# State-space layers: two more states weighed on TensorE and ScalarE, a block's first statistics on GpSimd, and the next decay first in each slot

## The chip, the cores and the metric

The kernel runs on one core of a Trainium2 chip, as one launch. The core has five engines that work beside each other, each through its own queue in order: TensorE (PE in the profile: matrix products and transposes, into PSUM), VectorE (DVE), ScalarE (ACT), GpSimd (POOL), and the sync engine (SP), which here only issues DMAs. The metric is the device time of the launch in microseconds (us), lower is better. The kernel before took 2108.87 us (median of three runs, 2108.46 to 2109.21).

## The reference, cut to what matters

The network has four layers of two halves each. The change is in one half only, the first half of layer 1 (names in l1a): four state-space layers one after another, on 4 sequences of 256 tokens (1024 columns after the batch is regrouped), with 256 inner channels and 16 states. In each of them:

```
xz = layer_norm(x) @ Wi.T;  xs, z = split(xz)
u  = silu(conv4(xs) + cb)
dt, Bc, Cc = split(u @ Wx.T);  dt = softplus(dt @ Wdt.T + bdt)
step t:  h = exp(dt[t]*A) * h + dt[t]*B[t]*u[t]      # 256 channels x 16 states
         y[t] = sum over states of h * C[t]
y = (y + u*Dp) * silu(z);  x = x + y @ Wo.T
```

All is float32. The 16 states of a channel are independent until the sum over states that gives y.

## The kernel before, in words

The tokens are worked on in four blocks of 512, and the four layers give 16 **blocks** in all (class Job, `jobs`; 128 channels lie on the partitions, two halves c of the channels, 512 tokens in the free dimension). A block has 16 **slots**, one for each state s. The loop over `slots` (L1077) writes the order of PE, DVE, ACT and POOL out by hand (`manual_schedule`); what stands before the loop is ordered by the scheduler. In slot s of a block:

- `decay` (L972, ACT, two instructions of 128x510) writes the decays of the *next* state into one of two PSUM buffers `das`; it waits until the scan two before has read that buffer.
- `inflow` (L966, POOL, 128x1024) makes the scan's input three slots ahead, in a buffer of the tag st; `weigh` (L999, POOL, the same size) multiplies a scanned state by its row of C.
- `scan` (L977, DVE) is the recurrence of the state, 128x1024, in place.
- The sum over states has two ways. An odd state is *turned* (`turn`, L986 to L993): half of its columns is transposed by four PE instructions into the single PSUM bank "acc", and two DVE instructions of 128x256 multiply by C, which is then a value per partition, and add into `yt`. One half is done one slot after the scan and one half two slots after, so that each slot has one set of four transposes and one pair of DVE instructions; for s = 1 ACT does them (L991). An even state is weighed by POOL and added on PE into the PSUM tile `yacc` (`add_up`, L1008, two matmuls of 128x512 with the identity); ADD gives the slot of that. State 8 is turned too, by EXTRA, through the bank "mm", in slot 10 and slot 0 of the next block. So nine states are turned and seven weighed. `tail` (L1010) adds `yt` into `yacc` by PE, multiplies by the gate and projects.
- `front` (L831) is the next but one block's preparation, a generator of some 40 steps. Two are taken per slot, from slot 6 of one block to slot 9 of the next: one at the head of the slot (before decay), one near its end. Its PE work stands in the second of a slot's steps, and ACT reads the result in the first step of the following slot. All go through one PSUM bank, "mm". By slot: statistics of the layer norm (DVE, slot 6) with two small VectorE instructions L849 and L850, then the reciprocal root on POOL (L854 to L859, slot 9), normalization (ACT L864, slot 10), transposes (PE L869, slot 11), the convolution as matmuls with shifted inputs (L880, in slots 12 and 13 for half the channels and 14 and 15 for the others), read by ACT (L885) in slots 14 and 0, Silu of u and of the gate with their table loads (L888, L949, slot 0), B, C and dt (L895 to L913, slots 1 to 4), z (L929, slots 5 and 6), and the softplus and dt*u (L936 to L943, slots 7 to 9).

Before the loop, block 0's front is run whole, the other blocks' outer layer norms are done, and at the loop's first pass block 1's front is started with 20 steps at once (L1081 to L1084).

PSUM has eight banks: one "mm", one "acc", two buffers of decays of two banks each, and `yacc` of two.

Of the kernel before, what the change touches and what calls it, by code (L numbers as in the profile page):

```python
# [9 lines left out]
F32 = mybir.dt.float32  # L10
BF16 = mybir.dt.bfloat16
U32 = mybir.dt.uint32
AF = mybir.ActivationFunctionType
ALU = mybir.AluOpType
AX = mybir.AxisListType

P = 128
B, S, D = 8, 256, 128
NTB = 4
TB = 512  # L20
# [4 lines left out]
NL, DI, DS, DR = 4, 256, 16, 8  # L25
# [5 lines left out]
EPS = 1e-5  # L31
# [143 lines left out]
def network_kernel(ctx: ExitStack, tc: tile.TileContext, x_in, packs, places, conv_w, out, stages=STAGES):  # L175
    nc = tc.nc
    V, A, G, T = nc.vector, nc.scalar, nc.gpsimd, nc.tensor
# [25 lines left out]
    xs = []  # L203
# [9 lines left out]
    for tb in range(1, NTB):  # L213
        load_x(tb)
    ident, ones, part, headmask, tri, run, iota, first = (
        K(n) for n in ("ident", "ones", "part", "headmask", "tri", "run", "iota", "first"))
# [7 lines left out]
    def layer_norm(src, name, dst=None):  # L224

        gen = norm(src, name, dst)
        while True:
            try:
                next(gen)
            except StopIteration as end:  # L230
                return end.value
# [52 lines left out]
    def ts(i, n=P):  # L284
        return slice(i * n, (i + 1) * n)
# [488 lines left out]
    def l1a(w0):  # L774
# [7 lines left out]
        LEAD = 26  # L782
        AHEAD = 3
        Q = 2
        with ExitStack() as es:
# [3 lines left out]
            pool = es.enter_context(tc.tile_pool(name="l1a", bufs=2))  # L789
            tmp = es.enter_context(tc.tile_pool(name="l1a_t", bufs=1))  # L790
            big = es.enter_context(tc.tile_pool(name="l1a_b", bufs=5))
# [39 lines left out]
            def front(job):  # L831
# [14 lines left out]

                rt = sm.tile([P, 4, NT], F32, tag="rt", name=f"rt_{n}")
                r0, v, t, nm = (rt[:, j] for j in range(4))
                V.tensor_scalar(v, mv[:, :, 1], EPS, None, ALU.add)  # L849
                V.tensor_scalar(nm, mv[:, :, 0], -1.0, None, ALU.mult)  # L850

                for _ in range(6):
                    yield
                G.tensor_tensor(r0, v, mhalf, ALU.pow)  # L854
                G.tensor_tensor(t, v, r0, ALU.mult)
                G.tensor_tensor(t, t, r0, ALU.mult)
                G.tensor_scalar(t, t, -0.5, 1.5, ALU.mult, ALU.add)
                G.tensor_tensor(r0, r0, t, ALU.mult)
                G.tensor_tensor(nm, nm, r0, ALU.mult)  # L859
                yield  # L860
                yield
                xn = tk.tile([P, NT, D], F32, tag="xn", name=f"xn_{n}")
# [98 lines left out]

            def inflow(job, s):

                job.st[s] = t = big.tile([P, 2, TB], F32, tag="st", name=f"st_{job.n}_{s}", bufs=14)
                row = job.rows_b[s // Q][:, s % Q, :]
                G.tensor_tensor(t, job.du, row.unsqueeze(1).to_broadcast([P, 2, TB]), ALU.mult)  # L966

            def decay(job, s):
                da = das[s % 2]
                for c in range(2):  # L970
                    k = c * DS + s
                    A.activation(seq(da[:, c, :])[:, :, 1:], seq(job.dt[:, c, :])[:, :, 1:], AF.Exp,  # L972
                                 scale=rates[job.l][:, k : k + 1])
# [2 lines left out]
                st = flat(job.st[s])  # L976
                V.tensor_tensor_scan(st, flat(das[s % 2]), st, 0.0, ALU.mult, ALU.add)  # L977

            def turn(job, s, half, kind="acc"):

                st = job.st[s]
                ps = mm_tile(f"tr_{job.n}_{s}_{half}", kind)
                for j in range(2):
                    i = 2 * half + j
                    for c in range(2):
                        T.transpose(ps[:, j * DI + c * P : j * DI + (c + 1) * P], st[:, c, ts(i)], ident)  # L986
                for j in range(2):
                    i = 2 * half + j
                    src, dst, cs = ps[:, ts(j, DI)], job.yt[:, i, :], job.ct[:, i, s : s + 1]
                    if s == 1:  # L990
                        A.activation(dst, src, AF.Copy, scale=cs)  # L991
                    else:
                        V.scalar_tensor_tensor(dst, src, cs, dst, ALU.mult, ALU.add)  # L993
# [34 lines left out]
            jobs = []  # L1028
# [8 lines left out]
            def slot(g):  # L1037
                return slots[g] if 0 <= g < len(slots) else (None, 0)

            layer_norm(xs[0], "l1a0", ys[0])  # L1040
            for _ in front(jobs[0]):
                pass
            for tb in range(1, NTB):
                layer_norm(xs[tb], f"l1a{tb}", ys[tb])

            def rows_of(g):

# [15 lines left out]

            EXTRA = {10: (0, 8, 0), 0: (1, 8, 1)}
            ADD = {0: 9, 2: 10, 4: 11, 6: 12, 10: 14, 12: 16, 14: 18}
            adds = {}
            for g, (job, s) in enumerate(slots):
                if s in ADD:  # L1070
                    adds[g - s + ADD[s]] = job, s
            gens, fronts = {}, []
            step = lambda what: next(gens.get(what, iter(())), None)

            kinds = mybir.EngineType
            with tc.manual_schedule(engines={kinds.PE, kinds.DVE, kinds.Activation, kinds.Pool}):
                for g in range(len(slots) + 10):  # L1077
                    job, s = slot(g)

                    nxt = slot(g + LEAD)  # L1080
                    if nxt[0] and (g == 0 or nxt[1] == 0):  # L1081
                        fronts.append(front(nxt[0]))
                        for _ in range(2 * nxt[1]):
                            next(fronts[-1])  # L1084
                    for gen in fronts:
                        next(gen, None)
                    if job:
# [4 lines left out]

                        rows_of(g + 3 * Q)
                        rows_from(g + 2 * Q)
                    nxt = slot(g + 1)
                    if nxt[0]:
                        decay(*nxt)
                    if slot(g + AHEAD)[0]:
                        inflow(*slot(g + AHEAD))
                    if job:  # L1100
# [6 lines left out]
                    if j2 and s2 in ADD:  # L1107
                        weigh(j2, s2)
                    at = g % DS
                    if at in EXTRA:  # L1110
                        j2 = slot(g - DS * EXTRA[at][0])[0]
                        if j2:
                            turn(j2, *EXTRA[at][1:], "mm")
                    if at == 7:
                        step("tail")
                    if job and s == 8:
# [446 lines left out]
```

## Time and profile before

| what | value |
|---|---|
| median of three runs | 2108.87 us |
| the profiled execution: its time, its span | 2106.59 us, 2104.8 us |
| busy share of the span: PE, DVE, ACT, POOL | 75%, 80%, 51%, 60% |
| first scan starts, last scan ends | 376.9 us, 1394.3 us |
| a block in the middle (705.4 to 769.0) | 63.6 us: DVE 60.2 busy, POOL 54.4, PE 46.3, ACT 41.7 |
| scans L977 | 256 of 2280 ns |
| turns' DVE instructions L993 | 512 of 469 ns |
| inflow L966, weighing L999 (POOL) | 256 of 2356 ns, 112 of 2355 ns |

The profile has one line for a group of instructions (source line, engine, operation, output and inputs by name, shapes, count, busy us and mean ns, idle time before them and what ended it). A timeline has one line for a run of like instructions: start, duration, engine, line, operation, tiles, count, and in brackets the idle time of that engine before it with what released it. A matmul in float32 that is no transpose is issued twice, so that a product of 128x512 has two rows. PE's busy time is modelled at the ends; the distance between starts says more. The time stands 1.8 us above the span in the profiled execution, and the median of the runs 2.3 us above that time.

### The profile page before, as it was taken

To read this page: it belongs to the slowest core of one execution; us is meant where nothing else is said; L and a number is where in the kernel's file an instruction comes from. 1 tells how busy PE (TensorE), PEld (TensorE's weight loads), DVE (VectorE), ACT (ScalarE), POOL (GpSimd) and SP (SyncE) were. 2 spreads that over 40 slices of the span, in tenths; PEclk is the share of its full clock that TensorE was granted. 3 is DMA by queue.
4 is the path that set the end of the run, shared out by engine and by line. 5 is a ranking of instruction groups with operands and counts; after the bars stand their busy time and mean duration, and the time that the engine had idled before them with its cause. 6 is when DMAs were issued, how large, how long until landed. Compare 5 with 4: busy or idle time off the path is not lost. (4 is left out here: it accounts for less than half of the span.)

```text
span 2104.8 us, 21141 instructions
## 1 busy us (share of the span) xinstructions
PE 1585.9 (75%) x6829; PEld 946.2 (45%) x6829; DVE 1674.1 (80%) x3020; ACT 1077.4 (51%) x1759; POOL 1257.9 (60%) x887
## 2 busy tenths in 40 slices
PE   4989875587767787777776668679999867694775
PEld 1434332243433443433443334444455667583665
DVE  6776446699999999999999999973555558799996
ACT  2655333675566765666755667433221335353442
POOL 1000002898889988889888899941242544837356
PEclk8999997688889888789888889799999989786887
DMA  4000002233223332233223333300020524320000
GB/s 127 1 1 1 0 29 91 90 102 113 99 92 123 102 107 95 92 113 112 102 98 95 105 103 104 108 0 0 0 72 13 185 92 158 91 73 9 6 6 5
DMA packets 67693, 153.27 MB, mean 73 GB/s; under 512 B 5248, under 2 KB 26368, under 8 KB 67328
## 3 DMA queue, kind: packets, MB, share of 16 engines
q1 hardware_dynamic: 60224, 123.79, 17.6%
q0 software_dynamic: 7360, 28.14, 4.2%
q8 instruction: 54, 0.88, 0.2%
q14 instruction: 55, 0.45, 0.1%
HBM read 142.74 MB, written 9.18 MB: 72 GB/s over the span
## 5 line engine op out<-in xcount | busy, mean ns | idle before, releaser
L977 DVE TENSOR_TENSOR_SCAN st_l1a<-da,st_l1a 128x1024 f32<-128x1024 f32 x256 | 582.3, 2280 | 56.5 <-ACT da L972 52.8
L966 POOL TENSOR_TENSOR st_l1a<-du_l1a,b_l1a 128x1024 f32<-128x1024 f32 x256 | 597.4, 2356 | 1.4 <-DVE du_l1a L941 1.4
L972 ACT ACTIVATE da<-dt_l1a,na 128x510 f32<-128x510 f32 x512 | 351.5, 689 | 153.3 <-DVE st_l1a L977 144.4
L986 PE MATMUL tr_l1a<-w_const,st_l1a 128*128 128x128 f32 x1152 | 203.8, 310 | 226.1 <-DVE yt_l1a L993 202.4
L999 POOL TENSOR_TENSOR st_l1a<-st_l1a,c_l1a 128x1024 f32<-128x1024 f32 x112 | 263.7, 2355 | 118.5 <-DVE st_l1a L977 118.3
L986 PEld LDWEIGHTS tr_l1a<-w_const,st_l1a 128*128 128x128 f32 x1152 | 151.5, 158 | 372.7 <-issue 214.4
L1008 PE MATMUL y_l1a<-st_l1a,w_const 128*128 128x512 f32 x448 | 238.6, 660 | 0.0
L993 DVE SCALAR_TENSOR_TENSOR yt_l1a<-tr_l1a,ct_l1a,yt_l1a 128x256 f32<-128x256 f32 x512 | 216.3, 469 | 12.1 <-PE tr_l1a L986 11.9
L626 PE MATMUL o_l0a<-ex_l0a,va_l0a 128*32 128x256 f32 x512 | 140.6, 401 | 1.9 <-ACT ex_l0a L618 1.7
L880 PE MATMUL u_l1a<-xp,cw 128*128 128x512 f32 x256 | 122.0, 601 | 2.4 <-ACT u_l1a L885 1.6
L1184 PE MATMUL h_l1f<-h_l1f,w_l1f 128*128 128x512 f32 x256 | 116.7, 592 | 0.0
L1008 PEld LDWEIGHTS y_l1a<-st_l1a,w_const 128*128 128x128 f32 x448 | 86.5, 215 | 63.9 <-issue 63.9
L618 ACT ACTIVATE ex_l0a<-s_l0a 128x512 f32<-128x512 f32 x128 | 75.3, 596 | 73.7 <-PE s_l0a L613 73.4
L1457 POOL TENSOR_TENSOR xd<-de,ex_l3f 128x1024 f32<-128x1024 f32 x32 | 65.2, 2058 | 61.2 <-ACT de L1452 61.1
L1492 PE MATMUL wT<-w_const,wa 128*128 128x128 f32 x512 | 73.5, 311 | 22.6 <-ACT wa L1473 17.0
L1188 ACT ACTIVATE h_l1f<-h_l1f,w_l1f 128x512 f32<-128x512 f32 x32 | 22.0, 687 | 120.9 <-PE h_l1f L1184 120.9
L1492 PEld LDWEIGHTS wT<-w_const,wa 128*128 128x128 f32 x512 | 71.2, 226 | 23.9 <-ACT wa L1473 17.4
L1459 POOL TENSOR_TENSOR xd<-xd,ey_l3f 128x1024 f32<-128x1024 f32 x32 | 78.7, 2477 | 0.2
L1240 POOL TENSOR_TENSOR st_l2a<-st_l2a,qk_l2a 128x512 f32<-128x512 f32 x32 | 40.4, 1269 | 63.0 <-DVE st_l2a L1239 53.5
L385 POOL DMA_INDIRECT we_l2f<-w_l2f,rows_l2f x44 | 47.3, 1074 | 48.9 <-PE y_l2f L418 31.6
L1184 PEld LDWEIGHTS h_l1f<-h_l1f,w_l1f 128*128 128x128 f32 x256 | 48.5, 190 | 60.3 <-issue 59.3
L626 PEld LDWEIGHTS o_l0a<-ex_l0a,va_l0a 128*32 128x32 f32 x512 | 47.1, 112 | 60.1 <-issue 34.1
(493 smaller groups left out, 3287.2 us busy)
## 6 DMA issues: line engine op xcount, KB each, us to landing
b_l1a<-rows_l1a SPq DMA_DIRECT2D x128, 512.0 KB, 3.6
c_l1a<-rows_l1a SPq DMA_DIRECT2D x64, 512.0 KB, 4.5
w_l1f<-w_l1f SPq DMA_DIRECT2D x1, 2888.0 KB
in_l2f<-zero SPq DMA_DIRECT2D x4, 704.0 KB, 7.1
w_l1a<-w_l1a SPq DMA_DIRECT2D x4, 572.0 KB, 6.2
cw<-conv_w SPq DMA_DIRECT2D x4, 512.0 KB
xt_l2f<-in_l2f SPq DMA_DIRECT2D x8, 256.0 KB
out_l2f<-yt_l2f SPq DMA_DIRECT2D x8, 256.0 KB, 3.3
```

The source lines that it names most:

```text
L626: T.matmul(po[b, g][32 * j : 32 * j + 32, :S], va[:, 2 * b + kc, h, :], ex[:, ts(kc, S)], start=kc == 0, stop=kc == 1)
L880: T.matmul(seq(ps), cw[:, j, ts(c)], xp[:, :, j : j + S], start=j == 0, stop=j == 3)
L966: G.tensor_tensor(t, job.du, row.unsqueeze(1).to_broadcast([P, 2, TB]), ALU.mult)
L972: A.activation(seq(da[:, c, :])[:, :, 1:], seq(job.dt[:, c, :])[:, :, 1:], AF.Exp, scale=rates[job.l][:, k : k + 1])
L977: V.tensor_tensor_scan(st, flat(das[s % 2]), st, 0.0, ALU.mult, ALU.add)
L986: T.transpose(ps[:, j * DI + c * P : j * DI + (c + 1) * P], st[:, c, ts(i)], ident)
L993: V.scalar_tensor_tensor(dst, src, cs, dst, ALU.mult, ALU.add)
L999: G.tensor_tensor(st, st, row.unsqueeze(1).to_broadcast([P, 2, TB]), ALU.mult)
L1008: T.matmul(job.yacc[:, c, :], ident, job.st[s][:, c, :], start=False, stop=False)
L1184: T.matmul(ps, w(wn)[:, k * HID + c * P : k * HID + (c + 1) * P], h[:, k, :], start=k == 0, stop=k == NC - 1)
L1459: G.tensor_tensor(xd, xd, wide(ey[:, rs].unsqueeze(2), 2, NX, NK), ALU.mult)
L1492: T.matmul(ps[:, ts(c)], wa[:, h, ts(c)], ident, start=h == 0, stop=h == NH - 1)
```

## The change

Five edits, all in l1a. (1) `front`: the two small VectorE instructions on the statistics (add EPS; negate the mean) are dropped; GpSimd adds EPS at the head of its root, and multiplies by -1 at its end. (2) In a slot, the next state's decay stands at the head, ahead of `front`'s first step. (3) State 10 is no longer weighed by GpSimd: ten states are turned. States 8 and 10 are now turned in another way: transposed by PE into "mm" (`across`), scaled from there by ACT into SBUF (`scaled`, four instructions of 128x256 for a state), and in the next slot transposed back by PE, as products with the identity that accumulate into `yacc` (`back`, eight matmuls of 128x128 for a state). Slots 10 and 11 do state 8, 12 and 14 state 10. The sum of state 12 moves from slot 0 to slot 15. (4) Block 1's first 20 front steps are taken before the loop, among the outer layer norms, where the scheduler orders them. (5) The tag st has 13 buffers, not 14.

```diff
@@ front
-                V.tensor_scalar(v, mv[:, :, 1], EPS, None, ALU.add)
-                V.tensor_scalar(nm, mv[:, :, 0], -1.0, None, ALU.mult)
                 for _ in range(6):
                     yield
+                G.tensor_scalar(v, mv[:, :, 1], EPS, None, ALU.add)
                 G.tensor_tensor(r0, v, mhalf, ALU.pow)
...
-                G.tensor_tensor(nm, nm, r0, ALU.mult)
+                G.tensor_tensor(nm, mv[:, :, 0], r0, ALU.mult)
+                G.tensor_scalar(nm, nm, -1.0, None, ALU.mult)
@@ inflow
-                job.st[s] = t = big.tile([P, 2, TB], F32, tag="st", name=f"st_{job.n}_{s}", bufs=14)
+                job.st[s] = t = big.tile([P, 2, TB], F32, tag="st", name=f"st_{job.n}_{s}", bufs=13)
@@ turn
-            def turn(job, s, half, kind="acc"):
-                st = job.st[s]
+            def across(job, s, half, kind):
                 ps = mm_tile(f"tr_{job.n}_{s}_{half}", kind)
                 for j in range(2):
-                    i = 2 * half + j
                     for c in range(2):
-                        T.transpose(ps[:, j * DI + c * P : j * DI + (c + 1) * P], st[:, c, ts(i)], ident)
+                        T.transpose(ps[:, j * DI + c * P : j * DI + (c + 1) * P], job.st[s][:, c, ts(2 * half + j)],
+                                    ident)
+                return ps
+
+            def scaled(job, s, half):
+                ps = across(job, s, half, "mm")
+                t = pool.tile([P, 2, DI], F32, tag="sc", name=f"sc_{job.n}_{s}_{half}")
+                for j in range(2):
+                    A.activation(t[:, j, :], ps[:, ts(j, DI)], AF.Copy, scale=job.ct[:, 2 * half + j, s : s + 1])
+                return t
+
+            def back(job, s, half, t):
+                for j in range(2):
+                    for c in range(2):
+                        T.matmul(job.yacc[:, c, ts(2 * half + j)], t[:, j, ts(c)], ident, start=False, stop=False)
+
+            def turn(job, s, half):
+                ps = across(job, s, half, "acc")
@@ before the loop
-            layer_norm(xs[0], "l1a0", ys[0])
-            for _ in front(jobs[0]):
-                pass
-            for tb in range(1, NTB):
+            for tb in range(NTB):
                 layer_norm(xs[tb], f"l1a{tb}", ys[tb])
+                if tb == 0:
+                    for _ in front(jobs[0]):
+                        pass
+                elif tb == LEAD // DS:
+                    fronts = [front(jobs[tb])]
+                    for _ in range(2 * (LEAD % DS)):
+                        next(fronts[0])
@@ the plan and the loop
-            EXTRA = {10: (0, 8, 0), 0: (1, 8, 1)}
-            ADD = {0: 9, 2: 10, 4: 11, 6: 12, 10: 14, 12: 16, 14: 18}
+            EXTRA = {10: (8, 0), 11: (8, 1), 12: (10, 0), 14: (10, 1)}
+            ADD = {0: 9, 2: 10, 4: 11, 6: 12, 12: 15, 14: 18}
...
-                    if nxt[0] and (g == 0 or nxt[1] == 0):
+                    if nxt[0] and nxt[1] == 0:
                         fronts.append(front(nxt[0]))
-                        for _ in range(2 * nxt[1]):
-                            next(fronts[-1])
+                    nxt = slot(g + 1)
+                    if nxt[0]:
+                        decay(*nxt)
                     for gen in fronts:
                         next(gen, None)
...
-                    nxt = slot(g + 1)
-                    if nxt[0]:
-                        decay(*nxt)
                     if slot(g + AHEAD)[0]:
                         inflow(*slot(g + AHEAD))
...
-                    if at in EXTRA:
-                        j2 = slot(g - DS * EXTRA[at][0])[0]
-                        if j2:
-                            turn(j2, *EXTRA[at][1:], "mm")
+                    if late:
+                        back(*late.pop())
+                    if job and s in EXTRA:
+                        late.append((job, *EXTRA[s], scaled(job, *EXTRA[s])))
```

More of the change, by code (lines that the diff above doesn't have):

```diff
@@ L1071, in l1a @@
                     adds[g - s + ADD[s]] = job, s
-            gens, fronts = {}, []
+            gens, late = {}, []
             step = lambda what: next(gens.get(what, iter(())), None)
```

## The prediction

> **What bounds the kernel now.** The page's busy shares come first, then its costliest groups.
>
> ```profile
> PE 1585.9 (75%) x6829; PEld 946.2 (45%) x6829; DVE 1674.1 (80%) x3020; ACT 1077.4 (51%) x1759; POOL 1257.9 (60%) x887
> ...
> L977 DVE TENSOR_TENSOR_SCAN st_l1a<-da,st_l1a 128x1024 f32<-128x1024 f32 x256 | 582.3, 2280 | 56.5 <-ACT da L972 52.8
> ...
> L993 DVE SCALAR_TENSOR_TENSOR yt_l1a<-tr_l1a,ct_l1a,yt_l1a 128x256 f32<-128x256 f32 x512 | 216.3, 469 | 12.1 <-PE tr_l1a L986 11.9
> ```
>
> VectorE is fullest, and in this stage (376.9 to 1394.3 us) it is busy 950 of 1017 us: it sets the pace of an average slot, one scan (2.21 us start to start) and one pair of turns (0.77), 2.97 us. But slots differ. So I walked one block (705.4 to 769.0) through the timelines of each engine; the mean lengths of the slots below are distances between scan starts over blocks 1 to 14.
>
> VectorE's timeline in slot 6, and GpSimd's beside it:
>
> ```profile
> 731.21 1.90 DVE L849 TENSOR_SCALAR rt_l1a<-mv_l1a 128x4 f32<-128x4 f32 x1
> 733.03 2.38 DVE L850 TENSOR_SCALAR rt_l1a<-mv_l1a 128x4 f32<-128x4 f32 x1
> 735.32 2.28 DVE L977 TENSOR_TENSOR_SCAN st_l1a<-da,st_l1a 128x1024 f32<-128x1024 f32 x1
> ```
> ```profile
> 730.73 2.35 POOL L999 TENSOR_TENSOR st_l1a<-st_l1a,c_l1a 128x1024 f32<-128x1024 f32 x1
> 733.03 2.35 POOL L966 TENSOR_TENSOR st_l1a<-du_l1a,b_l1a 128x1024 f32<-128x1024 f32 x1
> ```
>
> Two instructions of four elements take 4.1 us: each ends where a GpSimd instruction ends. With GpSimd idle (370.43 us, block 0) they took 0.17 and 0.16.
>
> TensorE's timeline in slots 12 to 14 of the same block:
>
> ```profile
> 757.35 0.63 PE L986 MATMUL tr_l1a<-w_const,st_l1a 128*128 128x128 f32 x4
> 757.82 1.88 PE L1008 MATMUL y_l1a<-st_l1a,w_const 128*128 128x512 f32 x4
> 759.53 1.88 PE L880 MATMUL u_l1a<-xp,cw 128*128 128x512 f32 x4
> 761.25 0.60 PE L986 MATMUL tr_l1a<-w_const,st_l1a 128*128 128x128 f32 x4
> 761.69 1.88 PE L880 MATMUL u_l1a<-xp,cw 128*128 128x512 f32 x4
> 763.41 0.60 PE L986 MATMUL tr_l1a<-w_const,st_l1a 128*128 128x128 f32 x4
> ```
>
> No bracket, so no idle: from slot 11 to slot 15 TensorE is as full as VectorE. By start distances at full clock: four transposes 0.44 us, a sum of a state 1.72, half a convolution 1.72, four back-products (as L1014, 722.65 to 723.65) 1.0.
>
> ScalarE's timeline at the block's slots 0 and 1:
>
> ```profile
> 706.35 0.69 ACT L885 ACTIVATE u_l1a<-u_l1a,w_l1a 128x512 f32<-128x512 f32 x1 [2.71 <-PE u_l1a L880]
> 706.94 1.41 ACT L972 ACTIVATE da<-dt_l1a,na 128x510 f32<-128x510 f32 x2
> 708.36 1.28 ACT L888 ACT_TABLE_LOAD   x1
> ...
> 711.68 1.28 ACT L972 ACT_TABLE_LOAD   x1
> 712.97 1.41 ACT L972 ACTIVATE da<-dt_l1a,na 128x510 f32<-128x510 f32 x2
> ```
>
> This is a second path: end of the convolution (PE, 706.15), its read, Silu twice with two table loads, decay of state 2 (to 714.38), scan of state 2 (714.49). It costs VectorE 2.1 us of idle in slot 1 on average.
>
> **The change part by part**, per block.
>
> *Statistics on GpSimd.* Within the stage L849 has 14 instances of 3772 ns and L850 about 0.6: 4.4 us each block leave slot 6 (mean length 8.5, with 2.97 of scan and turns and 1.2 of statistics). GpSimd pays 0.2 us twice (L857: 193 ns), beside 118 us of idle before its weighings. Here the Trainium skill speaks against the edit: Perfetto Trace Analysis, "Optimizing Scalar/DVE Operations", warns that moving work between VectorE and GpSimd might not help, as they share an SBUF port. By the rule nothing is gained, and my sum would be 62 us higher; the rows say that the wait is behind 2.35 us instructions of GpSimd, which its own queue doesn't pay again. I take the rows: **-4.4**.
>
> *VectorE's two extra turns of state 8* (slots 10 and 0) go: 2 x 0.77. That of slot 10 counts, **-0.8**; that of slot 0 lies within the stretch that follows.
>
> *States 8 and 10 by ScalarE and TensorE.* TensorE's slots, before and after:
> 11: 0.44+1.72+0.5 = 2.7; after, with back-products and transposes, +1.44 = 4.1.
> 12: 0.44+1.72+1.72 = 3.9; after +1.44 = 5.3.
> 13: 0.44+1.72 = 2.2; after +1.0 = 3.2.
> 14: 3.9; after, without state 10's sum, 0.44+0.44+1.72 = 2.6, plus two waits in the one bank "mm": its transposes wait 0.5 for ScalarE to read the convolution, and the next convolution waits 1.0 for ScalarE to read the transposes (pair 0.82 and two hand-overs of 0.1 to 0.2), 4.1.
> 15: 2.2; after, with back-products and state 12's sum, 4.9.
> Sum before 14.9, VectorE's five slots 14.85; after 21.6. The transposes may lag a scan by some 1.7 us (2.2 less their 0.5) before VectorE waits; that slack is spent at slot 12. The rest is idle of VectorE. And the second path starts when the convolution ends: 21.7 us after slot 11's scan start. From there to scan 2 it took 8.3 us; the decay of state 1 (1.4) now stands before the read, so 6.9. Stretch from scan 11 to scan 2: 28.7 against 23.9 (14.8+9.1): **+4.8**.
>
> ScalarE's own eight instructions (459 ns in L991's rows, no table load around those) are 3.7 us beside 129 us idle: nothing, while "mm" is the wait already counted; otherwise 0.8 a slot. GpSimd loses a weighing (2.36): nothing, it isn't late anywhere.
>
> *The clock.* In slots 10 and 11 TensorE was granted:
>
> ```profile
> 492.50:499.20 6.70, 5.57 (x24) 1.00 0.13 47
> ...
> 621.10:628.20 7.10, 6.85 (x19) 0.58 0.17 59
> ...
> 750.40:757.10 6.70, 6.46 (x24) 0.78 0.12 34
> ```
>
> (window, length, PE busy, granted clock.) Seven blocks of 14 have 1.00, four about 0.77, three 0.57. Before, slack took that up. Now slot 11's transposes start late and all behind them: 1.2 us in the second kind (free at 754.59 where, with 2.97 after scan 10 at 750.41, 753.4 is due), 2.2 in the third (2.6 us of work at half speed); (4 x 1.2 + 3 x 2.2)/14 = **+0.8**. The skill's TensorE: Matmul & The Clock Gate, "Why this matters for your kernels", would have the clock stay full where no idle gap exceeds some 3 us; the change removes idle, and by it this term would be 0. But the gaps in slots 8 and 9 (3.4 us ahead of 750.64, behind VectorE's dt*u and a scan) stay; I keep 0.8, bounds 0 and 2.2.
>
> *Decay first.* Its gain at state 1 is in the 6.9. Its price: front's reads stand 1.4 us later, and TensorE's next matmul in "mm" waits for them with slot transposes queued behind. In slot 3 the read of dt ends 5.0 to 5.2 us after scan 2's start (decay 1.35, copy 0.5, turn 0.7, decay 1.35, read 1.15), then dt's matmul 1.0, tail 1.0 to 1.9, transposes 0.6 to 1.0: 7.9 to 9.2 where scan 4 ends at 6.6. Idle 1.2 to 2.5 against 1.16 now: 0 to 1.4, taken **+0.8** (the clock in slot 4 is near half). In slot 7 z's copy behind a table load could add 0 to 0.5; I take none.
>
> *Buffers and queues.* With 13 buffers the inflow of slot 10 waits for the sum of slot 9; its scan is three slots (8.9 us) later, so nothing; uncovered, 2.4. On SP, a quarter of C's rows (states 8, 10) is still loaded though unread, and C's rows move up before B's; no buffer wait holds them, the rows are needed slots later (landing 4.5 us): nothing.
>
> *Block 1's first steps.* Scan 1 waited 10.5 us at 389.66 for a decay behind that front; scan 2 waits till 395.70 for Silu behind the same convolution. Moving one decay and the normalization ahead leaves that convolution (377.4 to 387.5) where it was in TensorE's queue, as the changed program's order shows: only the decay's 1.4 is gained: **-1.5** once.
>
> Sum: -4.4-0.8+4.8+0.8+0.8 = +1.2 for each of 14 blocks with a front, +16.8; the last two only lose turns, -3.1; prologue -1.5: +12.2. 2106.6+12.2 = 2118.8 for the profiled execution, +2.3 for the median: **2121 us**.
>
> **The rivals.** *TensorE is fast enough in slots 11 to 15* (the other side): the clock stays full, slot 14's waits vanish and dt's late read is covered. 4.8-1.5-0.8-4.4 = -1.9 a block, 14 x -1.9 - 4.6 = -31: 2078. It decides where the stretch, clock included, grows by less than 4.4 us. For: seven blocks are at full clock; against: 21.6 us of work by rows. *VectorE alone sets the pace* and all its savings arrive: 14 x 4.4 + 16 x 1.55 + 1.5 = 88 less, 2021; against: no idle in TensorE's rows. *The hand-overs ring*: "mm" passes delays from slot 7 and cold slots 10 on in every block: +2.6 more each, 2157; for: brackets in slots 3 to 7 already name ScalarE's reads.
>
> **How the numbers follow.** A measurement tells 0.2% (4.2 us) from no change. The case worked out (2105 to 2142 by the bounds): 0.64, of it 0.10 within 0.2%. First rival 0.20 (0.02 within), second 0.05, ringing 0.11. So slower 0.65, same 0.12, faster 0.23. The range 2082 to 2145 leaves out the second rival, the lower part of the first and most of the ringing, some 0.2.
>
> **What would show it.** Right: L849's 52.8 us gone with nothing in its place; slots 12 to 15 and 0 longer than 2.97, with VectorE idle ahead of the turns' instructions until PE's transposes, some 5 us a block; "DVE scan <- ACT da" still there at state 2; blocks near 65.8 us. Wrong: blocks of 60 us, TensorE idle between slots 11 and 15, or back-products far below 1.0 us for four.

## The result and the profile after

The changed kernel took 2162.19 us (median of four runs, 2158.63 to 2164.43), the kernel before, beside it on the same chip, 2109.04: a ratio of 1.0249, 95% interval 1.0231 to 1.0266. It is slower, as forecast, but by 53 us where 12 were worked out, and outside the range. The profiled execution took 2164.43 us (span 2162.7), 57.8 more than that of before.

The changed kernel's page, its engines' shares and three groups (the last fields: busy us, mean ns of one, idle of the engine before them and what ended it):

```profile
PE 1673.3 (77%) x7405; PEld 1027.9 (48%) x7405; DVE 1588.4 (73%) x2924; ACT 1133.0 (52%) x1887; POOL 1234.7 (57%) x903
...
L977 DVE TENSOR_TENSOR_SCAN st_l1a<-da,st_l1a 128x1024 f32<-128x1024 f32 x256 | 580.2, 2277 | 50.3 <-ACT da L972 47.7
...
L1011 DVE SCALAR_TENSOR_TENSOR yt_l1a<-tr_l1a,ct_l1a,yt_l1a 128x256 f32<-128x256 f32 x448 | 193.3, 473 | 145.2 <-PE tr_l1a L984 145.2
...
L993 ACT ACTIVATE sc_l1a<-tr_l1a,ct_l1a 128x256 f32<-128x256 f32 x128 | 53.7, 471 | 72.4 <-PE tr_l1a L984 72.4
```

VectorE does 86 us less and TensorE 87 us more. The turns' instructions on VectorE, which had 12.1 us of idle ahead of them, now have 145.2, all of it ended by TensorE's transposes; the scans' idle hardly moved. In those slots TensorE's queue sets the pace where VectorE did.

VectorE's timeline from slot 5 to the scan of slot 6 in a middle block:

```profile
691.10 0.86 DVE L843 BATCH_NORM_STATS2 st_l1a<-y 128x6 f32<-128x128 f32 x4
691.88 0.36 DVE L845 BATCH_NORM_AGGREGATE mv_l1a<-st_l1a 128x2 f32<-128x6 f32 x4
692.15 2.26 DVE L977 TENSOR_TENSOR_SCAN st_l1a<-da,st_l1a 128x1024 f32<-128x1024 f32 x1
```

The 4 us of L849 and L850 are gone and nothing stands in their place; GpSimd's own addition of EPS takes 227 ns on average. The gain arrives.

TensorE's timeline in slots 13 to 15 of the block that starts at 799.12:

```profile
859.58 1.06 PE L1000 MATMUL y_l1a<-w_const,sc_l1a 128*128 128x128 f32 x8
860.47 1.88 PE L880 MATMUL u_l1a<-xp,cw 128*128 128x512 f32 x4
...
863.13 0.66 PE L984 MATMUL tr_l1a<-w_const,st_l1a 128*128 128x128 f32 x4 [0.34 <-ACT u_l1a L885]
864.72 1.98 PE L880 MATMUL u_l1a<-xp,cw 128*128 128x512 f32 x4 [0.93 <-ACT sc_l1a L993]
866.54 0.60 PE L984 MATMUL tr_l1a<-w_const,st_l1a 128*128 128x128 f32 x4
```

Four back-products take 0.89 us from start to start (860.47 less 859.58; 1.0 was reckoned), and the two waits in the bank "mm" are the 0.34 and 0.93. VectorE in the same block, in slots 2 to 4 and then in slots 12 to 15:

```profile
809.48 6.65 DVE L977 TENSOR_TENSOR_SCAN st_l1a<-da,st_l1a 128x1024 f32<-128x1024 f32 x3 [2.55 <-ACT da L972]
819.45 0.88 DVE L1011 SCALAR_TENSOR_TENSOR yt_l1a<-tr_l1a,ct_l1a,yt_l1a 128x256 f32<-128x256 f32 x2 [3.31 <-PE tr_l1a L984]
```
```profile
854.58 0.88 DVE L1011 SCALAR_TENSOR_TENSOR yt_l1a<-tr_l1a,ct_l1a,yt_l1a 128x256 f32<-128x256 f32 x2 [0.85 <-PE tr_l1a L984]
859.78 0.88 DVE L1011 SCALAR_TENSOR_TENSOR yt_l1a<-tr_l1a,ct_l1a,yt_l1a 128x256 f32<-128x256 f32 x2 [2.13 <-PE tr_l1a L984]
867.18 0.88 DVE L1011 SCALAR_TENSOR_TENSOR yt_l1a<-tr_l1a,ct_l1a,yt_l1a 128x256 f32<-128x256 f32 x2 [1.28 <-PE tr_l1a L984]
```

Where the 57.8 us are, from the distances of scan starts (means over blocks 1 to 14 of one profiled execution each, in us):

| part of a block | before | after | difference | forecast |
|---|---|---|---|---|
| slots 11 to 15, 0 and 1 (the stretch) | 23.93 | 30.33 | +6.40 | +4.8 and +0.8 for the clock |
| slots 2 to 5 | 12.81 | 15.05 | +2.24 | +0.8 |
| slot 6 | 8.52 | 4.31 | -4.21 | -4.4 |
| slots 7 to 10 | 18.87 | 18.07 | -0.80 | -0.8 |
| sum | 64.13 | 67.76 | +3.63, x 14 = +50.8 | +1.2 |

To this come +11.9 for what stands before block 1 (the first scan starts 12.5 later, block 0 is 0.6 shorter), -1.6 in block 15, and -3.3 behind the loop.

### The profile page after: what moved, and what is told of

The parts are those of the page before. It is cut to its first block, busy times and chain, and to the rows that moved or that the text cites. A ratio compares the mean times of both kernels' runs of the same rounds, so it can differ in the third digit from the quotient of the medians.

```text
span 2162.7 us, 22293 instructions
## 1 busy us (share of the span) xinstructions
PE 1673.3 (77%) x7405; PEld 1027.9 (48%) x7405; DVE 1588.4 (73%) x2924; ACT 1133.0 (52%) x1887; POOL 1234.7 (57%) x903
## 5 line engine op out<-in xcount | busy, mean ns | idle before, releaser
L984 PE MATMUL tr_l1a<-w_const,st_l1a 128*128 128x128 f32 x1280 | 229.5, 313 | 147.0 <-DVE yt_l1a L1011 141.8
L1017 POOL TENSOR_TENSOR st_l1a<-st_l1a,c_l1a 128x1024 f32<-128x1024 f32 x96 | 226.4, 2358 | 192.9 <-DVE st_l1a L977 192.9
L984 PEld LDWEIGHTS tr_l1a<-w_const,st_l1a 128*128 128x128 f32 x1280 | 175.7, 163 | 293.0 <-issue 190.8
L1011 DVE SCALAR_TENSOR_TENSOR yt_l1a<-tr_l1a,ct_l1a,yt_l1a 128x256 f32<-128x256 f32 x448 | 193.3, 473 | 145.2 <-PE tr_l1a L984 145.2
L1026 PE MATMUL y_l1a<-st_l1a,w_const 128*128 128x512 f32 x384 | 219.0, 701 | 0.0
L1026 PEld LDWEIGHTS y_l1a<-st_l1a,w_const 128*128 128x128 f32 x384 | 77.2, 223 | 56.9 <-issue 56.9
L993 ACT ACTIVATE sc_l1a<-tr_l1a,ct_l1a 128x256 f32<-128x256 f32 x128 | 53.7, 471 | 72.4 <-PE tr_l1a L984 72.4
L885 ACT ACTIVATE u_l1a<-u_l1a,w_l1a 128x512 f32<-128x512 f32 x32 | 22.0, 688 | 120.1 <-PE u_l1a L880 120.1
L880 PEld LDWEIGHTS u_l1a<-xp,cw 128*128 128x128 f32 x256 | 47.2, 194 | 69.5 <-issue 45.3
L909 PE MATMUL dt_l1a<-xd_l1a,w_l1a 8*128 8x512 f32 x64 | 51.1, 889 | 37.1 <-ACT xd_l1a L898 20.2
```

What stands on the lines that cost most here:

```text
L880: T.matmul(seq(ps), cw[:, j, ts(c)], xp[:, :, j : j + S], start=j == 0, stop=j == 3)
L984: T.transpose(ps[:, j * DI + c * P : j * DI + (c + 1) * P], job.st[s][:, c, ts(2 * half + j)], ident)
L1017: G.tensor_tensor(st, st, row.unsqueeze(1).to_broadcast([P, 2, TB]), ALU.mult)
L1026: T.matmul(job.yacc[:, c, :], ident, job.st[s][:, c, :], start=False, stop=False)
```

## The experiments

Each kernel was timed beside the kernel before; the bracket is the 95% interval of the ratio. Slots and clocks are those of one profiled execution of each kernel. In a profile the granted clock is either 1.00 (full) or 0.50 (half; such stretches and slots are called cold), and it changes on a grid: the 150 stretches of one clock in the changed kernel's profile start whole multiples of 3.4133 us apart, to 0.002 us. The expectations call this grid the raster. "Loop" is the time from the first scan's start to the last scan's end in the profiled execution (1017.4 before, 1066.0 after).

### Each edit alone, on the kernel before

Edit 1 alone (diff: as in `front`).

> The kernel before with edit 1 alone (statistics on GpSimd). Theory (VectorE waited for GpSimd's instructions to end, and nothing is late behind it): slot 6 falls from 8.5 us to 4.2, 4.4 us in each of 14 blocks, 2109 - 62 = 2047 us. Rival (the shared port makes the move worth nothing, or GpSimd's or ScalarE's next wait takes the place): 2100 to 2109, with the wait back in slots 7 to 9.

Measured: 2062.22, ratio 0.9777 [0.9752, 0.9803]. Slot 6 falls from 8.52 to 5.10: 4.02 in all blocks but 2, 6 and 10, where another VectorE instruction, L823, stands in it (see the last experiment). The gain of the first edit holds.

Edit 2 alone (the decay moved to the head of the slot).

> The kernel before with edit 2 alone (decay first). Theory (two effects: state 2's decay 1.2 us earlier in slots 0 and 1; front's reads later, so that the slot's transposes in slots 3 to 5 wait behind dt's matmul at half clock, some 2 us): slots 0 and 1 together fall from 8.9 to 7.5, slots 3 to 5 rise from 10.6 to some 12.5, the sum +0.5 a block: 2109 + 7 = 2116, between 2105 and 2130. Rival (decay first is harmless, and slot 4's 6.3 us in the changed kernel come from states 8 and 10): slots 3 to 5 as before, 2109 - 18 = 2091.

Measured: 2111.34, 1.0005 [0.9992, 1.0019]. Slots 0 and 1 are 1.30 us shorter, slots 2 to 5 are 1.10 longer: gain and price cancel.

Edits 3 and 5 alone (`across`, `scaled`, `back`, EXTRA and ADD; 13 buffers).

> The kernel before with edits 3 and 5 alone (states 8 and 10 by ScalarE and TensorE, 13 buffers). Theory (slots 11 to 15 hold more TensorE work than VectorE's pace, and the Silu path starts when that work ends): slots 11 to 1 together rise from 23.9 us to some 30.5, slot 10 falls by 0.8: +6 a block, 2109 + 84 = 2193, between 2175 and 2215. Rival (the loss in the changed kernel is the order of the decays, not the products): below 2120.

Measured: 2208.83, 1.0469 [1.0449, 1.0488]. The stretch takes 32.07 us. This is the edit that loses.

Edit 4 alone (block 1's first steps ahead of the loop).

> The kernel before with edit 4 alone (block 1's first steps before the loop). Theory (VectorE's normalizations before the loop wait for GpSimd's roots, now twice as many, with layer 0's feed-forward work queued behind them): first scan 8 to 12 us later than at 376.9, scan 1 no longer late, together 2109 + 7 = 2116, between 2111 and 2122. Rival (the first scan's delay in the changed kernel comes from edit 1): first scan at 377, 2107.

Measured: 2116.93, 1.0041 [1.0026, 1.0056]: it costs 8 us where 1.5 were to be gained. The sum of the four, -46.9+2.3+99.7+7.8 = +63, is 10 more than all together.

### Each edit taken back, from the changed kernel

Without edit 4:

> The changed kernel with block 1's first steps back where they were in the kernel before (edit 4 undone). Theory (each edit's prologue delay is VectorE standing in its queue behind GpSimd's roots; alone edit 1 moved the first scan by 4.7 us and edit 4 by 6.8 us): the first scan comes at about 382 instead of 389.4, and the time falls by 7 to 8 us, to 2154 (2150 to 2158). Rival (the prediction's term, edit 4 gains 1.5 us and the loss in front of the loop is edit 1's alone): 2163 to 2165.

Measured: 2156.81 (2146.58 to 2166.08), 1.0231 [1.0183, 1.0280]. The first scan starts at 377.2, earlier than the 382 of the theory, but the time's interval overlaps that of the changed kernel: inconclusive for the whole. The four runs of this one program lie in two pairs, 2146.58 and 2148.94 at a mean granted clock of 0.87, 2164.68 and 2166.08 at 0.86; so the same instructions can take some 17 us more, with the clock granted lower.

Without edit 2:

> The changed kernel with the next decay back behind the front's first step (edit 2 undone). Theory (in the changed kernel decay first delays dt's two matmuls by a decay each and costs 2.2 us in slots 2 to 5, against the 1.4 us that it gains at state 1's decay): slots 2 to 5 fall from 15.05 to about 12.9 us, slot 1 grows by 1.3, together -0.9 a block: 2150 (2143 to 2158). Rival (the prediction's terms, 0.8 lost against 1.4 gained): 2170 (2166 to 2175).

Measured: 2169.82, 1.0277 [1.0258, 1.0295]; the theory's number fails. Slots 2 to 5 do fall to 13.05 (-2.0), but slots 0 and 1 take 1.35 more and slots 11 to 15 0.4 more, so the mean of a block stays (67.77). Per block the edit is neutral; its price sits in other slots than its gain. Whole, the kernel without it is 7.6 us slower, near the rival's 2170 but not by the rival's terms: block 0 is 4.3 us longer, and 3.6 lie behind the loop.

Without edits 3 and 5:

> The changed kernel with states 8 and 10 handled as in the kernel before (edits 3 and 5 undone; edits 1, 2 and 4 stand). Theory (TensorE is overfull in slots 11 to 15 only by the back-products and transposes of edit 3, and the other three add up as they did alone: 2062.2 + 2.3 + 7.8): 2072 (2064 to 2082), slots 11 to 15 at 2.97 each. Rival (the edits disturb each other through the one bank of the front, so the loss does not go with edit 3): above 2090.

Measured: 2089.97, 0.9891 [0.9867, 0.9915]. It is outside the theory's range and at the edge of the rival's: edit 3 costs 72 us beside the others, not 90. The stretch is back at 23.3, but its slots 11 and 13 last 3.3 and 3.5 in most blocks, and slot 7 is 1.0 longer there. Ordinary blocks last 61.42 to 61.44.

### TensorE's work, and its clock

Changed kernel without back-products:

```diff
-                    if late:
-                        back(*late.pop())
```

> The changed kernel without the eight back-products each of states 8 and 10 that add their scaled, turned states to the block's sum (this leaves the share of these two states out of the result; their transposes and ScalarE's scaling stay). It takes four times 0.89 us of TensorE's work out of slots 11 to 15. Theory (TensorE is overfull there): slots 11 to 15 fall from 20.06 to about 17.3 us (17.0 of work instead of 20.6, and the waits of slot 14 in the front's one bank stay), 14 blocks by 2.8: 2123 (2112 to 2135). Rival (the loss is the waits in the one bank, which TensorE's queue passes on, and not its work): less than 1 us a block, 2148 or more.

Measured: 2109.98, 0.9995 [0.9980, 1.0011]. Slots 11 to 15 fall from 19.96 to 17.15 (-2.8, as the theory has it), slots 0 and 1 by another 0.9 (the last back-products reach into slot 0), together 3.7 for 3.6 us of work. TensorE is overfull in the stretch. But the clock has a share in the 3.7: it rose from 0.62 to 0.77 in slots 9 to 11. In blocks at full clock in slots 10 and 11 the stretch lasts 28.6 us in the changed kernel (block 1) and 26.2 here (six blocks), so the work itself counts for 2.4 of its 3.6.

More work for TensorE ahead of slots 9 to 11:

```diff
@@ open_sum
-                for c in range(2):
-                    T.matmul(job.yacc[:, c, :], diags[job.l][:, c, :], job.u[:, c, :], start=True, stop=False)
+                for again in (True, False):
+                    for c in range(2):
+                        T.matmul(job.yacc[:, c, :], diags[job.l][:, c, :], job.u[:, c, :], start=True, stop=again)
@@ tail
-                for i in range(NT):
+                for i in (*range(NT), *range(NT)):
```

> The changed kernel with two groups of TensorE's matmuls done twice with the same result (the opening of a block's sum in slot 8, and the out-projection of the block before in slot 7), so that TensorE idles less ahead of slots 9 to 11. Clock theory (the half clock in slots 9 to 11 follows from the idle stretches of slots 6 to 9; block 1, at full clock there, is 2.3 us shorter in slots 11 to 15): the granted clock of slots 10 and 11 rises to about 1.00 in most blocks, slot 11 falls from 3.80 to 3.0 and slot 12 by 0.7; 10 to 12 blocks by 2.3: 2137 (2128 to 2148). Rival (the clock there is only a bystander, the work of slots 11 to 15 alone decides): 2162 or, with the added matmuls in the way, up to 2185.

Measured: 2161.17, 1.0242 [1.0225, 1.0259]: no change, the rival's number. Yet the granted clock in slots 9 to 11 rose from 0.62 to 0.87 and slots 11 to 15 became 1.35 us shorter: the clock is no bystander there. Slot 7, with the doubled out-projection, took 0.98 more, which used up most of that. (The profiled execution, 2155.78, is 5 us below the other three.)

More work ahead of slots 3 and 4:

```diff
-                for c in range(2):
+                for c in (0, 1, 0, 1):
                     T.matmul(ps[:NX, :], wd[:, c * NX : (c + 1) * NX], u[:, c, :], start=c == 0, stop=c == 1)
```

> The changed kernel with the product that gives dt, B and C's rows (slot 1 to 2, TensorE) done twice with the same result, while ScalarE is busy with two decays and reads it only afterwards. Theory (decay first costs more than its 1.4 us of delay because TensorE runs dry in slot 2, and dt's second matmul then takes 2.07 us at half clock where 1.0 was reckoned): the granted clock of slots 3 and 4 rises, and slot 4 falls from 6.30 by 1.0 to 1.5 us, less up to 0.5 by which the doubled product is late: 2150 (2141 to 2158). Rival (the delay by the decays alone makes slot 4 long): slot 4 stays within 0.3 us of 6.3, 2160 to 2168.

Measured: 2163.05, 1.0252 [1.0231, 1.0273]: no change. The clock in slots 3 and 4 rose from 0.57 to 0.78 and slots 2 to 5 fell from 15.05 to 14.07, so the theory's mechanism is there, at 1.0 us. In the three blocks with full clock in slots 3 and 4, slot 4 lasts 4.09 us and not 6.37, although the decays stand first in them too. Slot 7, where nothing was added, grew by 1.1. In both kernels the filling matmuls raised the clock in the slots that follow them, and most of the gain was lost in slot 7; why slot 7 grew here was not looked into.

### Where block 1's first steps stand

```diff
-            for tb in range(NTB):
+            layer_norm(xs[0], "l1a0", ys[0])
+            for _ in front(jobs[0]):
+                pass
+            for tb in range(1, NTB):
                 layer_norm(xs[tb], f"l1a{tb}", ys[tb])
...
+            fronts = [front(jobs[LEAD // DS])]
+            for _ in range(2 * (LEAD % DS)):
+                next(fronts[0])
```

> The changed kernel with block 1's first steps behind the normalizations of all four blocks, not between them (still ahead of the loop, and with the first decay ahead of them). Theory (VectorE stands in its queue behind GpSimd's roots of block 1, ahead of layer 0's last work): the first scan returns from 389.4 to 377 to 380, scan 2 from 405.95 to 394 to 397, and the time falls by some 9 us to 2153 (2146 to 2162). Rival (block 1's convolution and its reads ahead of the loop are what costs, wherever they stand): the first scan stays at 386 or later, 2158 to 2165.

Measured: 2163.60, 1.0264 [1.0243, 1.0284]: no gain. The place of the wait is as the theory has it (from the outer norms' first group, L257, to L716 it is 5.4 us, as before, and 9.3 in the changed kernel), but the first scan starts only at 384.9, scan 2 at 402.6: 3.9 us of the wait came back, 4.5 of the first scan's delay. What was won is lost behind the loop (711.6 us against 707.2), where the programs are alike. That stretch lay between 706.6 and 715.1 us in the twenty profiles, so two times can differ by several us that are not the loop's.

### A little more and a little less work for VectorE

Four changed kernels differ only in how many of the four statistics instructions (L843) of a front are done; the diff is the range of that loop, and where fewer are done, the results are shared out.

> The changed kernel with one of the four statistics instructions of a block's front (VectorE, slot 5; L843: 4 in 0.86 us), its result used for all four tiles, so the normalization of three tiles is left wrong. Slot 5 to 6 loses 0.6 us of VectorE's work. Sum theory: every block with a front is 0.6 us shorter, 67.6 instead of 68.25, 2154 (2151 to 2157). Raster theory (TensorE's cold windows stand at fixed places of the clock's 3.413 us raster, and a block that comes earlier meets them later in its own course): blocks stay at 68.25, and a wait elsewhere in the block grows by 0.6: 2160 to 2165.

> The changed kernel with two of the four statistics instructions of a block's front, each result used for two tiles (the normalization of two tiles is left wrong): about 0.3 us less of VectorE's work a block. Sum theory: 14 times 0.3 less, 2158 (2155 to 2161). Raster theory: the ordinary blocks are either still held at 68.25 us (2160 to 2165), or fall to 64.85, 19 windows, as with one instruction (2134 to 2142); nothing between by small steps.

> The changed kernel with six statistics instructions instead of four (two of them done twice with the same result): about 0.4 us more of VectorE's work a block. Sum theory: 14 times 0.4 more, 2168 (2165 to 2171). Raster theory: either held at 68.25 (2159 to 2165), or blocks that leave the raster's place with cold slots 9 to 11 and vary between 66 and 68, as with eight instructions: 2150 to 2160.

> The changed kernel with the four statistics instructions of a block's front done twice with the same result (VectorE, slot 5): 0.8 us more of VectorE's work. Sum theory: every block with a front is 0.8 us longer, 69.0, 2173 (2170 to 2177). Raster theory: blocks stay at 68.25 with a wait in the block shorter by 0.8 (2159 to 2166), or, where there is no such wait to eat up, go to 21 windows, 71.7 (over 2190).

| statistics | time, ratio | slot 6 | loop | slots 11 to 13 above 10.8, blocks 1 to 13 | granted clock, slots 9 to 11 |
|---|---|---|---|---|---|
| 1 | 2136.47, 1.0143 [1.0126, 1.0160] | 4.00 | 1038.3 | 4.9 us, in 3 blocks | 0.82 |
| 2 | 2147.54, 1.0177 [1.0155, 1.0198] | 4.09 | 1048.3 | 12.9 us, in 6 | 0.77 |
| 4 (changed kernel) | 2162.19, 1.0249 [1.0231, 1.0266] | 4.31 | 1066.0 | 27.2 us, in 12 | 0.62 |
| 6 | 2150.95, 1.0195 [1.0171, 1.0220] | 4.67 | 1048.2 | 7.7 us, in 5 | 0.83 |
| 8 | 2157.25, 1.0233 [1.0216, 1.0250] | 5.36 | 1058.8 | 9.5 us, in 7 | 0.81 |

Six instructions are faster than four (the intervals lie apart) and one saves 25.7 us where the sum theory has 8; eight are not told from four. So the sum theory is out. The raster theory is out in its strict form too (there are values between); what remains is how often a block meets the half clock in slots 10 to 12. Slots 11 to 13 last 10.8 us in a block at full clock, 13.3 where slot 11 is cold through, 12.1 where it is cold in part. One statistics instruction saves 14 x 0.31 = 4.3 us of slot 6 and 22.3 of cold slots, 26.6 in sum, and its loop is 27.7 shorter.

Stretches of the changed kernel and, second, of the kernel with one statistics instruction (start and end, length, busy us of PE, PEld, DVE, ACT and POOL, granted clock, share of DMA, GB/s):

```profile
634.69:644.93 10.24, 7.78 (x18) 3.93 (x17) 9.48 (x9) 5.60 (x11) 6.93 (x4) 0.50 0.36 116
...
702.96:713.20 10.24, 7.77 (x18) 3.94 (x17) 9.47 (x9) 5.60 (x11) 6.93 (x3) 0.50 0.32 115
...
771.22:781.46 10.24, 7.76 (x18) 3.94 (x17) 9.47 (x9) 5.60 (x11) 6.92 (x3) 0.50 0.34 111
```
```profile
950.58:960.82 10.24, 6.77 (x11) 2.24 (x9) 10.07 (x13) 3.43 (x6) 9.75 (x11) 0.50 0.32 114
...
1015.43:1025.67 10.24, 6.74 (x11) 2.26 (x9) 10.07 (x13) 3.45 (x6) 9.75 (x11) 0.50 0.16 51
```

In the changed kernel the half-clock stretch comes back every 68.26 us, to 0.02 us, at the same place of each block: it ends 3.0 us into slot 11 (scan 11 starts at 641.93). In the other it comes every 64.85 us and ends before slot 10 (scan 10 at 961.19).

### The decay first in slot 0 only

In the changed kernel (`nxt` goes to the head only if s is 0, else it stays behind the front's first step), and in the kernel before with edit 1:

> The changed kernel with the next decay first in slot 0 only; in slots 1 to 15 it stands behind the front's first step as in the kernel before. Theory (edit 2 gains 1.35 us in slots 0 and 1 by one decay, and loses 2.0 us in slots 2 to 5 by others): slots 0 and 1 stay at 10.4 us, slots 2 to 5 fall from 15.05 to 13.1, 14 blocks by 2.0: 2134 (2124 to 2146). Rival (the loss of slots 2 to 5 is not edit 2's but that of the late end of the stretch before, so it stays): 2158 to 2170.

> The kernel before with edit 1, and with the next decay first in slot 0 only (the decay of state 1 ahead of the convolution's read; all other slots as before). Theory (decay first gains at state 1 and costs at dt's matmuls in slots 2 to 4, so the one can be had without the other): slots 0 and 1 fall from 8.9 to 7.6 us as with edit 2 alone, slots 2 to 5 stay at 13.0, so 15 blocks by 1.2 less than edit 1 alone (2062): 2045 (2038 to 2053). Rival (what is gained at state 1 is given back by a TensorE that is then cold or late elsewhere, as in the three edits together at 2090): 2060 to 2075.

Measured: 2141.63, 1.0145 [1.0126, 1.0165], and 2041.66, 0.9682 [0.9664, 0.9699]. In the first, slots 0 and 1 stay (10.41), slots 2 to 5 fall to 12.74 (-2.3) and slot 6 grows by 0.3: 20.6 us of the 53 come back with it. The second is 20.6 better than edit 1 alone (its loop is 17.7 shorter); its slots 0 and 1 take 7.56, as with edit 2 alone, at no price in slots 2 to 5 (12.89). Its ordinary blocks last 58.03.

### What is left in slot 6

In that kernel, VectorE in block 6, and GpSimd beside it:

```profile
766.87 6.79 DVE L823 TENSOR_TENSOR cw<-cw,w_l1a 128x1024 f32<-128x1024 f32 x1
```
```profile
767.90 2.36 POOL L999 TENSOR_TENSOR st_l1a<-st_l1a,c_l1a 128x1024 f32<-128x1024 f32 x1
770.23 2.34 POOL L966 TENSOR_TENSOR st_l1a<-du_l1a,b_l1a 128x1024 f32<-128x1024 f32 x1
772.65 1.08 POOL L852 TENSOR_SCALAR rt_l1a<-mv_l1a 128x4 f32<-128x4 f32 x1
```

The same instruction took 1.2 to 1.3 us in the kernel before, 1.78 in the changed kernel's block 6 and 4.85 in block 2 of edit 1 alone. The last kernel gives it to GpSimd (V to G in L823):

> The kernel before with edit 1, the decay first in slot 0 only, and the product of the next layer's taps (L823, three times in the loop, 128 x 1024) on GpSimd instead of VectorE. Theory (VectorE's instruction ends with GpSimd's: slot 6 of blocks 2, 6 and 10 takes 9.9 to 10.7 us there and 4.02 in all others): the three slots fall to 4.0 to 4.5 us, by 6 us each: 2023 (2017 to 2030). Rival (GpSimd's queue, which takes the product's 2.4 us or more, is then late for the products of dt*u that the scans wait for): 2033 to 2045.

Measured: 2034.58, 0.9658 [0.9642, 0.9675], the lowest median of all, though the interval overlaps that of the kernel without this step; GpSimd does it in 2.34 us. Slot 6 is 4.15 as the theory has it, but slot 7 of the three blocks grows to between 7.8 and 9.0, and with it goes much of the gain. The time is the rival's, its mechanism is not what block 6 shows: VectorE sits idle there for 1.35 us ahead of the turn until TensorE's transposes, and TensorE before them for 3.73 until ScalarE has read z.

## Why the prediction was right or wrong

The sum was 45.6 us short (57.8 measured, 12.2 worked out). Three terms failed: the price of decay first (2.24 a block for 0.8, 20.2 us in 14 blocks), block 1's first steps (+11.9 for -1.5, 13.4 us), and the clock, with which the stretch is 0.80 a block longer than the sum (11.2 us). Slot 6 is 2.7 us short of its gain, and the last blocks and the part behind the loop give 1.8 back. That the direction was right is in part luck: the 12.2 are less than either of the first two errors, and all three happened to go the same way.

- **Statistics on GpSimd**: right, -4.21 for -4.4. The rows beat the rule of the skill's Perfetto Trace Analysis that was weighed against them: alone the edit gives 46.9 us. It falls short of the 62 there because L823 then stands longer in slot 6 of three blocks.
- **The turn of slot 10**: right, -0.80.
- **The stretch at full clock**: right. Block 1 of the changed kernel, at 1.00 in slots 10 and 11, has 18.2 us in slots 11 to 15 and 10.4 in 0 and 1, 28.6, where 28.7 was worked out; the convolution ends 21.7 after scan 11's start, as in the text. That TensorE's work makes the stretch longer is shown, for 2.4 us of it, by leaving the back-products out.
- **The clock**: the mechanism was right, the size was not. The term took over how often blocks of the kernel before are cold there, 7 of 14 in all degrees. In the changed kernel 12 of 13 are, at up to 2.5 us: 30.33-28.6 = 1.7 a block for 0.8. The rule of the Trainium skill's TensorE: Matmul & The Clock Gate, "Why this matters for your kernels", by which the term would have been 0, does not hold here: in a block of 68.25 us (594.34 to 662.59) the longest idle between matmuls is 2.60 us, and yet TensorE has half clock for 23.9 us, where the block of before that was walked (705.4 to 769.0) has idle of 7.25 and 3.41 us and half clock for 13.7. How many blocks meet the cold stretch moves by a third of a microsecond of work, which no sum over slots gives.
- **Decay first**: the largest step that failed. The gain was right (1.3 to 1.35; 1.4), the price was not (2.0 to 2.3 for 0.8). The walk from scan 2 holds up to one step. Forecast: read of dt ends 5.0 to 5.2 after scan 2's start; measured 4.95 (814.43 less 809.48). Then dt's matmul was put at 1.0, as in the block of before that was walked:

```profile
718.17 1.12 PE L909 MATMUL dt_l1a<-xd_l1a,w_l1a 8*128 8x512 f32 x2 [0.50 <-ACT dt_l1a L913]
```

In the changed kernel it took 2.07 at a granted clock of 0.50:

```profile
814.48 2.07 PE L909 MATMUL dt_l1a<-xd_l1a,w_l1a 8*128 8x512 f32 x2 [0.96 <-ACT dt_l1a L913]
816.48 2.08 PE L1032 MATMUL y_l1a<-w_const,yt_l1a 128*128 128x128 f32 x8
818.35 1.06 PE L984 MATMUL tr_l1a<-w_const,st_l1a 128*128 128x128 f32 x4
```

The tail's products behind it (1.87 from start to start) and the transposes were within their bounds. The text had said that the clock of slot 4 is near half, gave both rows behind it their half-clock ends, and left this one at full clock; so the idle of 3.31 us lies outside its 1.2 to 2.5. (Its terms add up to 7.6 to 9.1, not 7.9 to 9.2, which changes little.) These slots are also colder than in the kernel before: there dt's second matmul is at half clock in 4 of the blocks 1 to 14, with edit 2 alone (granted clock 0.77 in slots 3 and 4, price 1.10) in 2, in the changed kernel (0.57) wholly in 12. In the three blocks at full clock of the kernel with the rows' product done twice, slots 2 to 5 last 12.57, no more than before: what decay first costs there, it costs by the half clock.
- **Block 1's first steps**: failed in sign. Alone the edit costs 7.8 us where 1.5 were to be gained. What was foreseen, the convolution staying where it is and the decay's gain, came: from scan 0 to scan 2 it is 2.3 us less (-1.5). What was not asked is what stands behind the moved steps in queues that run other work. VectorE before the loop, in the kernel before and then in the changed kernel:

```profile
332.76 1.12 DVE L257 TENSOR_SCALAR y<-x,mv_l1a,rs_l1a 128x128 f32<-128x128 f32 x4 [3.38 <-POOL rs_l1a L251]
...
338.17 0.95 DVE L716 TENSOR_TENSOR h_l0f<-gs_l0f,u_l0f 128x352 f32<-128x352 f32 x2 [0.30 <-ACT gs_l0f L711]
...
359.66 0.69 DVE L731 TENSOR_TENSOR x<-x,d_l0f 128x512 f32<-128x512 f32 x1 [6.67 <-PE d_l0f L729]
```
```profile
335.63 1.11 DVE L257 TENSOR_SCALAR y<-x,mv_l1a,rs_l1a 128x128 f32<-128x128 f32 x4 [4.71 <-POOL rs_l1a L251]
...
343.55 1.11 DVE L257 TENSOR_SCALAR y<-x,mv_l1a,rs_l1a 128x128 f32<-128x128 f32 x4 [4.72 <-POOL rs_l1a L251]
344.94 0.95 DVE L716 TENSOR_TENSOR h_l0f<-gs_l0f,u_l0f 128x352 f32<-128x352 f32 x2 [0.28 <-ACT gs_l0f L711]
...
372.50 0.69 DVE L731 TENSOR_TENSOR x<-x,d_l0f 128x512 f32<-128x512 f32 x1 [11.48 <-PE d_l0f L729]
```

L716 is the layer before, still at work; it now stands behind two waits for GpSimd, in whose queue block 1's eight root instructions (337.89 to 340.96) come ahead of the second norm's. From the first L257 row to L716 it is 9.3 us (5.4 before), from there to L731 27.6 (21.5 before; 23.1 with edit 4 alone, where L729's twenty matmuls take 2.50 us as before, and not 4.21 at half clock as here). With the 2.3 back, and 0.3 between L731 and the first scan, 7.4 us at scan 2. The other 2.9 lie ahead of the first L257 row, where kernels without the edit differ by up to 5.0; that was not looked into. Of all this, the 3.9 us ahead of L716 are shown to come of the queue's order (they go when block 1's steps stand last); the 6.1 between L716 and L731 are explained by the half clock only in part. With edit 4 the first scan starts anywhere from 381.5 to 391.1 in the profiles (384.9 with block 1's steps last), without it from 376.9 to 381.6.
- **The last two blocks**: block 15 loses 1.6 as forecast; block 14 still carries the end of a front and is 3.6 longer.

The rival "the hand-overs ring" gave nearly the time (2157), by luck: slots 7 to 10 are as the sum had them, so no delay is passed on from slot 7, and in slots 13 to 15 the bank "mm" costs only 0.34 and 0.93, which were in the sum as 0.5 and 1.0. What is right in it is that cold slots 10 on cost more than the sum had. What the runs leave open is why the cold stretches keep their place in a block: that they do is shown, what holds them is not. A hint: in blocks 1 to 13 of the changed kernel each of the 38 grid steps of 3.413 us ahead of a fall to half clock has TensorE's matmuls busy for at most 0.62 of it, and each of the 38 ahead of a return for at least 0.87. But steps after which the clock stayed full go down to 0.42, so this share alone does not decide.

## What to carry to other kernels

Moving work off the fullest engine pays only if the one that takes it has room in those very slots: sum the taker's work slot by slot, at the clock granted there, half clock included. When steps are moved, list what stands behind them in every in-order queue, also of the stage before. And a reordering that gains at one place and pays at others is worth having at the one place only (edit 2 in slot 0 only: 20.6 us faster than in every slot of the changed kernel, and 20.6 faster than in no slot of the kernel before with edit 1).

## What was not expected of the hardware

In some kernels the length of blocks without L823 settles on whole multiples of 3.413 us, the grid on which the granted clock changes in the traces (the Trainium skill, TensorE: Matmul & The Clock Gate, "What's actually happening", has a free-running activity window of 3413 ns; the spacing agrees): 68.26 (20), 64.85 (19), 61.43 (18) and 58.03 (17) in four kernels. In others, such as those with six and eight statistics instructions or with edit 1 alone, the blocks vary. So the time is not monotonic in the work: twice the statistics, 1.05 us a block more in slot 6, cost nothing (1.0233 against 1.0249), and half of them less gave 14.7 us.

A VectorE instruction's duration depended on what GpSimd ran beside it, and not for small ones only: L823 took 1.2 to 1.3, 1.78, 4.85 and 6.79 us in four kernels, and 2.34 on GpSimd itself. The Trainium skill's SBUF — State Buffer, "Who interferes with whom", has it that a VectorE instruction with two inputs in SBUF contends with a GpSimd instruction that reads SBUF, and that the order of issue decides who blocks. In the row of 6.79 us two whole ones, started after it, pass by (767.90 to 772.57) before it ends, so here the earlier start did not decide. Then GpSimd's next, L852, takes 1.08 where it took 0.23 in the changed kernel, and ends with it (773.73 and 773.66). Why the same instruction is held so much longer in one kernel than in another was not looked into.
